# The last twelve batches of a gathered low-rank residual kernel, written out as one list

## The chip, the cores and the metric

The kernel runs on one core of a Trainium2 chip. Time is the device time of one execution in microseconds (us); the median of three runs before the change is 304.21 us (304.19 to 304.54). A core has a matrix engine (TensorE, PE in the profile), VectorE (DVE), ScalarE (ACT), GpSimd (POOL) and SyncE (SP), each with an instruction queue of its own, and 16 DMA engines. SBUF is the on-chip memory, PSUM the eight banks into which TensorE writes.

## The reference: what is computed

Each of B = 128 batches has S = 128 rows of H = 512 numbers and an index that picks one of L = 10 parameter sets.

```python
w1 = W1[language_ids]                                   # 512 x 128 for each batch
w2 = W2[language_ids]                                   # 128 x 512
h = relu(einsum('bsh,bha->bsa', x, w1) + b1[ids])
y = x + einsum('bsa,bah->bsh', h, w2) + b2[ids]
normed = (y - mean(y)) * rsqrt(var(y) + 1e-5)           # over H
out = x + normed * gamma[ids] + beta[ids]
```

Everything is float32.

## The kernel before, in words

One batch is one tile of 128 partitions (its rows) by 512 columns. x is loaded four batches at a time, results are stored two at a time (tile o). A batch b passes through these steps, each a function of the kernel:

- `transpose_x` (TensorE, four 128x128 transposes into PSUM) and `copy_xT` (ScalarE, back to SBUF);
- `stage_w1` (ScalarE, copies the batch's W1 from the ten that stay in SBUF into a small tile, because the index is known only on the chip);
- `down` (TensorE, four products) and `relu` (ScalarE);
- `up` (TensorE, one product of 512 columns into one of five PSUM banks, `py`);
- `add_b2` and `add_beta` (GpSimd: r = x + b2, o = x + beta). For some batches VectorE (`vector_b2`) or, for the last two, TensorE adds b2 instead;
- `residual` (VectorE: py += r, with the row sum as a by-product) and `square` (ScalarE: sum of squared deviations);
- `scalar_means` and `deviation` (ScalarE: minus the mean, and an approximate 1/sqrt, the root, into a PSUM bank that rotates), then `rstd` in three small VectorE steps that sharpen the root by Newton's method. Means, roots and rstd are made for two batches (a pair) at once;
- `scale` (VectorE: (py - mean) * gamma) and `finish` (VectorE: py * rstd + o, into o), then `store` (SyncE).

The function `keep` makes each engine issue in exactly the order in which the code is written, so the text is the schedule. The main loop (line 577) writes one batch per turn, with the stages of about five batches interleaved: x is turned two batches ahead, a batch is finished about two behind. With E = 123, batches 124 to 127 are handled by `tail(b)` (line 463): there mean, root and rstd are made for one batch alone (`deviation_of`, `rstd_of`, `of_one` with the roots of 126 and 127 in PSUM banks of the finished stages), and the ends of 123, 124 and 125 leave VectorE: `by_pool` lets ScalarE make n = py * rstd + shift and GpSimd multiply by gamma (for 123 and 124) and add it to o. 125 to 127 are stored singly or in halves, some of it from ScalarE's queue (`store_last`).

Of the kernel before, what the change touches and what calls it, by code (L numbers as in the profile page):

```python
# [26 lines left out]
def cond_resid_kernel(ctx: ExitStack, tc: tile.TileContext, x, itok, W1, b1, W2, b2, gamma, beta, out):  # L27
# [112 lines left out]
    def lid(b, engine):  # L140
        g = b // G
        if (g, engine) not in lids:
            loads, vals = nc.values_load_multi_w_load_instructions(
                lang[0:1, g * G : (g + 1) * G],
                engines=[engine],
                min_val=0,
                max_val=L - 1,
                skip_runtime_bounds_check_because="clamped on the chip to 0..L-1 above",
            )
# [164 lines left out]
    def col(tiles, b):  # L314

        return tiles[b // 2][:, b % 2 : b % 2 + 1]
# [43 lines left out]
    def root(ssq, t):  # L360
        keep(nc.scalar.activation(t, ssq, AF.Abs_reciprocal_sqrt, bias=eps, scale=1.0 / H3))  # L361

    def newton(n, ssq, t, u):
        if n == 1:
            keep(nc.vector.scalar_tensor_tensor(u, ssq, EPS * H3, t, ALU.add, ALU.mult))  # L365
        else:
            keep(nc.vector.scalar_tensor_tensor(u, u, 1.0 / H3, t, ALU.mult, ALU.mult))

    def newton_3(rstd, t, u):
        keep(nc.vector.scalar_tensor_tensor(rstd, u, -3.0, t, ALU.add, ALU.mult))  # L370
# [28 lines left out]
    def finish(b):  # L399
        g, j = divmod(b, 2)  # L400
        o = os[g][:, j, :]
        keep(
            nc.vector.scalar_tensor_tensor(o, ys.pop(b), rstds[g][:, j : j + 1], o, ALU.mult, ALU.add)  # L403
        )

    def store(g):
        keep(nc.sync.dma_start(out=out[2 * g : 2 * g + 2].rearrange("b s h -> s b h"), in_=os.pop(g)))
        del rstds[g]

    def on(b):  # L410
        return 0 <= b < B
# [3 lines left out]
    shifts = {}  # L415
    halves = slice(0, H // 2), slice(H // 2, H)

    def of_one(b):
        if -b not in parts_of:
            pool, tag = {E + 3: (p_h, "h"), E + 4: (p_x, "xT")}.get(b, (p_s, "s"))  # L420
            parts_of[-b] = pool.tile([P, 1], FP, tag=tag, name=f"root_of_{b}"), st.tile([P, 1], FP, tag="part", name=f"part_of_{b}")
        return parts_of[-b]

    def rstd_of(b, n):

        t, u = of_one(b)
        if n < 3:
            newton(n, ssqs[b], t, u)
        else:
            rstds[b] = st.tile([P, 1], FP, tag="rstd", name=f"rstd_{b}")  # L430
            newton_3(rstds[b], t, u)

    def deviation_of(b):
        ssqs[b] = st.tile([P, 1], FP, tag="ssq", name=f"ssq_{b}")
        sq = tp.tile([P, H], FP, tag="sq", name=f"sq_{b}")
        keep(nc.scalar.activation(sq, ys[b], AF.Square, bias=col(sums, b), scale=-float(H), accum_out=ssqs[b]))  # L436
        root(ssqs[b], of_one(b)[0])

    def rstd_col(b):
        return rstds[b] if b > E else rstds[b // 2][:, b % 2 : b % 2 + 1]  # L440
# [5 lines left out]
    def by_pool(b, scaled, cols=slice(0, H)):  # L446

        n = rp.tile([P, H], FP, tag="r", name=f"n_{b}")[:, cols]
        bias = 0.0 if scaled else shifts[b]
        keep(nc.scalar.activation(n, ys[b][:, cols], AF.Identity, bias=bias, scale=rstd_col(b)))  # L450
        if not scaled:
            keep(nc.gpsimd.tensor_tensor(n, n, gamma_b[:, bass.ds(lid(b, ET.Pool) * H, H)], ALU.mult))
        for part in halves if b > E else (cols,):
            keep(nc.gpsimd.tensor_tensor(os[b // 2][:, b % 2, part], n[:, part], os[b // 2][:, b % 2, part], ALU.add))
# [4 lines left out]
    def finish_cols(b, cols=slice(0, H)):  # L459
        o = os[b // 2][:, b % 2, cols]  # L460
        keep(nc.vector.scalar_tensor_tensor(o, ys[b][:, cols], rstd_col(b), o, ALU.mult, ALU.add))  # L461

    def tail(b):
        p = E // 2
        residual(b)
        if b == E + 1:
            rstd(p, 1)
            scale(E - 1)
            rstd(p, 2)
            finish(E - 2)  # L470
            store(p - 1)
            rstd(p, 3)
            deviation_of(b)
            shift(E)
            by_pool(E, False)
        elif b == E + 2:
            rstd_of(b - 1, 1)
            negative_means(b // 2)
            rstd_of(b - 1, 2)
            finish_cols(E - 1)  # L480
            store_last(E - 1)
            rstd_of(b - 1, 3)
            store_last(E)
            deviation_of(b)
        elif b == E + 3:
            left, right = slice(0, H // 2), slice(H // 2, H)
            few, most = slice(0, H // 4), slice(H // 4, H)
            shift(b - 2)
            by_pool(b - 2, False)
            residual(b + 1)  # L490
            rstd_of(b - 1, 1)
            scale(b - 1)
            rstd_of(b - 1, 2)
            deviation_of(b)
            negative_means(b // 2)
            scale(b)
            rstd_of(b - 1, 3)
            rstd_of(b, 1)
            deviation_of(b + 1)
            rstd_of(b, 2)  # L500
            by_pool(b - 1, True)
            for part in halves:
                store_last(b - 2, nc.scalar, part)
            for part in halves:
                store_last(b - 1, nc.scalar, part)
            rstd_of(b, 3)
            rstd_of(b + 1, 1)
            finish_cols(b)
            store_last(b)
            rstd_of(b + 1, 2)  # L510
            scale(b + 1)
            rstd_of(b + 1, 3)
            for cols in (left, right):
                finish_cols(b + 1, cols)
                store_last(b + 1, nc.sync, cols)


    def spin(n, width):
        idle = p_s.tile([P, H], FP, tag="s", name="idle")
# [54 lines left out]
    up(1)  # L574

    turned = 5
    for i in range(3, B + U):
        b = i - U - 1
        if b > G and b % G == 2 and b // G + 3 < NG and b // G + 3 >= 5:
            load_x(b // G + 3)  # L580
        up_to = i
        if b <= E:
            if turned <= up_to and on(turned):
                transpose_x(turned)
            add_b2(b + 2)
# [18 lines left out]
        if b == E:  # L604
            add_b2(b + 3)
            add_beta(b + 1)
            add_b2(b + 4)
            for n in range(b + 2, B):
                add_beta(n)
        if b > E:  # L610
            tail(b)
        elif half == 0:
            if on(b):
                vector_b2(b)
                residual(b)
                square(b)
            if mine:
                scale(2 * p)
                rstd(p, 1)
            if old:  # L620
                finish(2 * p - 1)
                store(p - 1)
        else:
            if on(b):
                vector_b2(b)
            if mine:
                rstd(p, 2)
            if on(b):
                residual(b)
                square(b)  # L630
            if mine:
                rstd(p, 3)
                scale(2 * p + 1)
            if mine:
                finish(2 * p)
        if 0 <= g and b <= E and half == 1:
            scalar_means(g)
            deviation(g)

        for n, engine in ((turned + 2, ET.Activation), (i - U + 3, ET.PE), (b + 1, ET.DVE), (b + 6, ET.Pool)):  # L640
            if on(n):
                lid(n, engine)


# [35 lines left out]
```

## Time and profile before

| | |
|---|---|
| median of three runs | 304.21 us |
| the profiled execution | 304.08 us, its span 302.3 us |
| busy share of the span | TensorE 96%, VectorE 97%, ScalarE 92%, GpSimd 94% |
| granted TensorE clock | 0.993 on the mean |
| HBM traffic | 43.3 MB read, 33.6 MB written, 254 GB/s over the span |
| one turn of the loop (from one `up` to the next) | 2.19 us |
| last `up` starts, last VectorE instruction ends, span ends | 292.40, 299.20, 302.3 us |

Times in views count from the start of the span. The busy shares are averages over the whole run; what bounds the end must be read from the end. A busy time is that of an instruction from its start to its end; on VectorE the next one starts some 0.09 us before the one ahead has ended, so the cost of an instruction to its engine is the distance from its start to the next start. "SPq" and "ACTq" are the queues of SyncE and ScalarE that issue transfers.

### The profile page before, as it was taken

How to read it: one execution, taken by the hardware profiler on the slowest of the kernel's cores; microseconds unless marked ns; L12 is line 12 of the kernel's file. 1: busy time of each engine (PE TensorE's matmuls, PEld its weight loads, DVE VectorE, ACT ScalarE, POOL GpSimd, SP SyncE). 2: the span in 40 equal slices, each digit the busy share in tenths (PEclk: the TensorE clock that was granted, in tenths of full speed). 3: DMA queues.
4: the chain of work that ended last, by engine and by line, in shares of the span. 5: the costliest groups of instructions: out<-in, count | busy, mean ns of one | idle time of the engine just before them, and what ended most of it. 6: DMA issues, size and time to landing. Idle time of an engine off the chain costs nothing.

```text
span 302.3 us, 7001 instructions
## 1 busy us (share of the span) xinstructions
PE 290.6 (96%) x1820; PEld 218.0 (72%) x1821; DVE 294.2 (97%) x784; ACT 279.6 (92%) x771; POOL 284.9 (94%) x240
## 2 busy tenths in 40 slices
PE   7899999999999999999999999999999999999980
PEld 3758787777777777777777777777777777777740
DVE  6989999999999999999999999999999999999995
ACT  5878789999999999999999999999999999999982
POOL 1299998999999999999999999999999999999995
PEclk9999999999999999999999999999999999999997
DMA  6999999986667876766678667767866666882244
GB/s 235 385 389 364 346 339 402 404 307 206 233 234 243 279 255 205 244 209 261 222 280 270 212 204 240 263 226 261 279 211 221 218 253 217 271 283 113 108 166 173
DMA packets 43929, 77.33 MB, mean 256 GB/s; under 512 B 2121, under 2 KB 8020, under 8 KB 43890
## 3 DMA queue, kind: packets, MB, share of 16 engines
q1 hardware_dynamic: 43254, 76.31, 73.5%
q10 hardware_dynamic: 636, 0.57, 0.6%
q8 instruction: 15, 0.25, 0.3%
q14 instruction: 24, 0.20, 0.2%
HBM read 43.32 MB, written 33.55 MB: 254 GB/s over the span
## 4 chain that ended last, share of the span: by engine, by line
PE 89%; DVE 5%; DMA 2%; issue 1%; ACT 1%; SPq 0%; POOL 0%; DVEq 0%; ACTq 0%; POOLq 0%
PE ph L294 36%; PE py L311 35%; PE pxT L271 18%; DMA x<-in_x_dram 2%; DVE py L394 2%; DVE py L328 1%; DVE o L403 1%; PE row L229 1%; SPq L161 0%; ACT n L450 0%; ACT sq L351 0%; ACT sq L436 0%; DVE o L461 0%; ACT w1s L262 0%; DVE rstd L370 0%
## 5 line engine op out<-in xcount | busy, mean ns | idle before, releaser
L288 POOL TENSOR_TENSOR o<-x,beta_b 128x512 f32<-128x512 f32 x128 | 170.1, 1359 | 12.7 <-DVE beta_b L247 11.6
L294 PE MATMUL ph<-xT,w1s 128*128 128x128 f32 x1024 | 135.3, 275 | 0.2 <-DMA w1s<-in_L_cond_W_dram 0.2
L281 POOL TENSOR_TENSOR r<-x,b_b 128x512 f32<-128x512 f32 x97 | 131.7, 1360 | 0.0
L311 PE MATMUL py<-w,hT 128*128 x256 | 131.3, 595 | 0.0
L294 PEld LDWEIGHTS ph<-xT,w1s 128*128 128x128 f32 x1024 | 124.8, 192 | 1.3 <-issue 0.6
L271 PEld LDWEIGHTS pxT<-ident,x 128*128 128x128 f32 x512 | 66.0, 149 | 66.8 <-issue 49.9
L394 DVE SCALAR_TENSOR_TENSOR py<-py,nmean,gamma_b 128x512 f32<-128x512 f32 x126 | 94.8, 753 | 0.0
L403 DVE SCALAR_TENSOR_TENSOR o<-py,rstd,o 128x512 f32<-128x512 f32 x122 | 91.1, 747 | 0.0
L351 ACT ACTIVATE sq<-py,sum 128x512 f32<-128x512 f32 x124 | 85.8, 692 | 0.6 <-DVE py L328 0.6
L275 ACT COPY xT<-pxT 128x512 f32<-128x512 f32 x128 | 74.7, 583 | 4.3 <-PE pxT L271 4.1
L271 PE MATMUL pxT<-ident,x 128*128 128x128 f32 x512 | 77.6, 274 | 0.8 <-DMA x<-in_x_dram 0.6
L262 ACT COPY w1s<-w 128x512 f32 x111 | 68.0, 613 | 0.0
L328 DVE SCALAR_TENSOR_TENSOR py<-py,r 128x512 f32<-128x512 f32 x97 | 66.9, 690 | 0.2
L302 ACT ACTIVATE hT<-ph,b1T 128x128 f32<-128x128 f32 x128 | 46.9, 367 | 8.8 <-PE ph L294 4.2
L311 PEld LDWEIGHTS py<-w,hT 128*128 128x128 f32 x256 | 39.1, 192 | 1.4 <-issue 0.7
L351 ACT ACTIVATION_READ_ACCUMULATOR sq<-py,sum 128x1 f32 x124 | 25.1, 202 | 0.0
L328 DVE SCALAR_TENSOR_TENSOR py<-py,x 128x512 f32<-128x512 f32 x31 | 21.7, 699 | 1.4 <-PE py L311 1.1
L321 DVE TENSOR_TENSOR py<-py,b_b 128x512 f32<-128x512 f32 x27 | 18.6, 689 | 0.1
L361 ACT ACTIVATE root<-ssq,eps 128x2 f32<-128x2 f32 x62 | 16.5, 265 | 0.0
L328 DVE DVE_READ_ACCUMULATOR py<-py,r 128x1 f32 x97 | 13.6, 140 | 0.0
L342 ACT ACTIVATE nmean<-sum 128x2 f32<-128x2 f32 x62 | 12.3, 198 | 0.0
L365 DVE SCALAR_TENSOR_TENSOR part<-ssq,root 128x2 f32<-128x2 f32 x62 | 9.3, 149 | 0.2 <-ACT root L361 0.2
(57 smaller groups left out, 81.2 us busy)
## 6 DMA issues: line engine op xcount, KB each, us to landing
out_dram<-o SPq DMA_DIRECT2D x61, 512.0 KB, 3.3
x<-in_x_dram SPq DMA_DIRECT2D x27, 1024.0 KB, 6.7
x<-in_x_dram SPq DMA_DIRECT2D x10, 512.0 KB, 7.2
w1s<-in_L_cond_W_dram SPq DMA_DIRECT2D x17, 256.0 KB, 8.7
w<-in_L_cond_W_dram SPq DMA_DIRECT2D x4, 640.0 KB, 8.2
w<-in_L_cond_W_dram SPq DMA_DIRECT2D x1, 1792.0 KB, 9.8
w<-in_L_cond_W_dram SPq DMA_DIRECT2D x1, 768.0 KB, 5.3
out_dram<-o SPq DMA_DIRECT2D x3, 256.0 KB, 2.0
```

Of the source, the lines that this page charges most:

```text
L262: keep(nc.scalar.copy(w1s[b].rearrange("p k a -> p (k a)"), src))
L271: keep(nc.tensor.transpose(pxs[b][:, k, :], cols, ident))
L275: keep(nc.scalar.copy(xT[b], pxs.pop(b)))
L281: keep(nc.gpsimd.tensor_tensor(rs[b], xb(b), b2_b[:, bass.ds(v * H, H)], ALU.add))
L288: keep(nc.gpsimd.tensor_tensor(os[g][:, j, :], xb(b), beta_b[:, bass.ds(v * H, H)], ALU.add))
L294: nc.tensor.matmul(phs[b], lhsT=w1s[b][:, k, :], rhs=xT[b][:, k, :], start=(k == 0), stop=(k == KC - 1))
L302: keep(nc.scalar.activation(hT[b], phs.pop(b), AF.Relu, bias=b1T[:, bass.ds(lid(b, ET.Activation), 1)]))
L311: keep(nc.tensor.matmul(ys[b], lhsT=hT[b], rhs=w2[:, bass.ds(v * H, H)], start=not m, stop=True))
L328: nc.vector.scalar_tensor_tensor(ys[b], ys[b], 1.0, r, ALU.mult, ALU.add, accum_out=col(sums, b))
L351: nc.scalar.activation(sq, ys[b], AF.Square, bias=col(sums, b), scale=-float(H), accum_out=col(ssqs, b))
L394: nc.vector.scalar_tensor_tensor(ys[b], ys[b], col(nmeans, b), gamma_b[:, bass.ds(v * H, H)], ALU.add, ALU.mult)
L403: nc.vector.scalar_tensor_tensor(o, ys.pop(b), rstds[g][:, j : j + 1], o, ALU.mult, ALU.add)
```

## The change

The loop stops after batch 121 has been turned (`range(3, B - 6)`), `tail` goes, and what is left of the twelve batches 116 to 127 is written out as one list of single steps, each on its engine. The work of a batch and the number of VectorE's large instructions stay; these parts change:

- the order of all steps from there on, TensorE's, ScalarE's, VectorE's, GpSimd's and SyncE's; the loads of the indices into registers (`lid`) for the last batches stand together ahead of the list;
- W1 of 125, 126 and 127 comes from HBM by the batch's index (`load_late`, SyncE) instead of by ScalarE's copy;
- by ScalarE and GpSimd go the ends of 120 and 124 (`n_of`, `gamma_of`, `add_of`) instead of 123 and 124; 122 and 123 are ended by VectorE as a pair;
- 125: VectorE writes (py - mean) * gamma to SBUF (`scale_out`), ScalarE makes a diagonal matrix of rstd (`diag_of`), TensorE puts x + beta into a PSUM bank (`base_of`: a product that picks beta's row, and x times the identity) and adds diag times n to it (`product_of`), ScalarE copies the bank to o (`copy_out`);
- 127: x + beta comes from TensorE in the same way and VectorE's last instruction reads it from PSUM;
- the roots of 125 and 126, not of 126 and 127, lie in banks of the finished stages; the means of 124 and 125 are made singly by VectorE, those of 126 and 127 by ScalarE;
- all stores go through SyncE: 120 to 123 as pairs, 124 in halves, 126 and 125 whole, 127 in halves.

```diff
-    for i in range(3, B + U):
+    for i in range(3, B - 6):
...
+    def base_of(b, pool, tag):
+        base[b] = pool.tile([P, H], FP, tag=tag, name=f"base_{b}")
+        pick_b = pick[:, bass.ds(lid(b, ET.PE), 1)].to_broadcast([96, P])
+        keep(nc.tensor.matmul(base[b], lhsT=pick_b, rhs=parts[:96, :], start=True, stop=False))
+        keep(nc.tensor.matmul(base[b], lhsT=ident, rhs=xb(b), start=False, stop=True))
+
+    def end_of(b, cols=slice(0, H)):
+        o = out_of(b)[:, cols]
+        keep(nc.vector.scalar_tensor_tensor(o, (rs if b in base else ys)[b][:, cols], rstd_col(b), base[b][:, cols] if b in base else o, ALU.mult, ALU.add))
...
+        if engine is nc.scalar:
+            keep(nc.scalar.activation(diags[b], ident, AF.Identity, scale=rstd_col(b)))
...
+    def product_of(b, cols=slice(0, H)):
+        keep(nc.tensor.matmul(base[b][:, cols], lhsT=diags[b], rhs=rs[b][:, cols], start=False, stop=True, skip_group_check=True))
+
+    def copy_out(b, cols=slice(0, H)):
+        keep(nc.scalar.copy(out_of(b)[:, cols], base[b][:, cols]))
+
+    def load_late(b):
+        w1s[b] = wp.tile([P, KC, A], FP, tag="w1s", name=f"w1s_{b}")
+        src = W1[bass.ds(lid(b, ET.SP), 1)].rearrange("o (k p) a -> p (o k) a", k=KC)
+        keep(nc.sync.dma_start(out=w1s[b], in_=src))
...
+    lid(E - 3, ET.DVE)
+    lid(E + 1, ET.DVE)
+    lid(E + 1, ET.PE)
+    lid(E + 1, ET.SP)
+    rstd(E // 2 - 3, 2)
+    transpose_x(E - 1)
+    b2_of(E - 2)
+    down(E - 2)
+    up(E - 3)
+    copy_xT(E - 1)
+    residual(E - 4)
+    square(E - 4)
+    rstd(E // 2 - 3, 3)
+    relu(E - 2)
...
+    b2_of(E + 2)
+    load_late(E + 2)
...
+    residual(E + 1)
+    up(E + 2)
+    rstd(E // 2, 3)
+    end_of(E - 1)
+    residual(E + 2)
+    square_of(E + 1)
+    root_of(E + 1)
+    down(E + 4)
+    rstd_of(E + 1, 1)
+    rstd_of(E + 1, 2)
+    square_of(E + 2)
+    up(E + 3)
+    mean_of(E + 1, nc.vector)
+    rstd_of(E + 1, 3)
+    shift(E + 1)
+    end_of(E)
+    relu(E + 4)
+    up(E + 4)
+    mean_of(E + 2, nc.vector)
+    n_of(E + 1, False)
+    residual(E + 3)
+    scale_out(E + 2)
+    root_of(E + 2)
+    store_pair(E // 2 - 1)
+    square_of(E + 3)
+    root_of(E + 3)
+    mean_of(E + 3, nc.scalar)
+    rstd_of(E + 2, 1)
+    residual(E + 4)
+    store_pair(E // 2)
+    rstd_of(E + 2, 2)
+    rstd_of(E + 3, 1)
+    gamma_of(E + 1)
+    add_of(E + 1, halves[0])
+    rstd_of(E + 2, 3)
+    diag_of(E + 2, nc.scalar)
+    rstd_of(E + 3, 2)
+    base_of(E + 2, p_y, "y")
+    add_of(E + 1, halves[1])
+    square_of(E + 4)
+    scale(E + 3)
+    mean_of(E + 4, nc.scalar)
+    store_last(E + 1, nc.sync, halves[0])
+    base_of(E + 4, p_y, "y")
+    rstd_of(E + 3, 3)
+    end_of(E + 3)
+    product_of(E + 2)
+    store_last(E + 1, nc.sync, halves[1])
+    store_last(E + 3, nc.sync)
+    root_of(E + 4)
+    rstd_of(E + 4, 1)
+    copy_out(E + 2)
+    store_last(E + 2, nc.sync)
+    rstd_of(E + 4, 2)
+    scale_out(E + 4)
+    rstd_of(E + 4, 3)
+    end_of(E + 4, halves[1])
+    store_last(E + 4, nc.sync, halves[1])
+    end_of(E + 4, halves[0])
+    store_last(E + 4, nc.sync, halves[0])
```

More of the change, by code (lines that the diff above doesn't have):

```diff
@@ L463, in tail @@
[L463 to L515, printed above, removed]
@@ L603, in cond_resid_kernel @@
         mine, old = 0 <= p < B // 2, 0 <= p - 1 < B // 2
[L604 to L612, printed above, removed]
+        if half == 0:
             if on(b):
@@ L642, in cond_resid_kernel @@
                 lid(n, engine)
+    lid(E - 3, ET.DVE)
[12 more added lines that the diff above has]
+    relu(E - 2)
+    deviation(E // 2 - 2)
+    b2_of(E + 2)
+    load_late(E + 2)
+    transpose_x(E)
+    scale(E - 6)
+    end_of(E - 7)
+    residual(E - 3)
+    stage_w1(E)
+    beta_of(E - 1)
@@ new lines, in cond_resid_kernel @@
+    scalar_means(E // 2 - 2)
+    copy_xT(E)
+    rstd(E // 2 - 2, 1)
+    end_of(E - 6)
+    scale(E - 5)
+    down(E - 1)
+    up(E - 2)
+    rstd(E // 2 - 2, 2)
+    beta_of(E + 1)
+    load_late(E + 3)
+    transpose_x(E + 1)
+    relu(E - 1)
+    down(E)
+    stage_w1(E + 1)
+    copy_xT(E + 1)
+    transpose_x(E + 2)
+    load_late(E + 4)
+    b2_of(E - 1)
+    scale(E - 4)
+    rstd(E // 2 - 2, 3)
+    beta_of(E - 2)
+    square(E - 3)
+    b2_of(E)
+    store_pair(E // 2 - 3)
+    up(E - 1)
@@ new lines, in cond_resid_kernel @@
+    relu(E)
+    residual(E - 2)
+    end_of(E - 5)
+    end_of(E - 4)
+    copy_xT(E + 2)
+    down(E + 1)
+    square(E - 2)
+    up(E)
+    residual(E - 1)
+    transpose_x(E + 3)
+    scalar_means(E // 2 - 1)
+    deviation(E // 2 - 1)
+    rstd(E // 2 - 1, 1)
+    rstd(E // 2 - 1, 2)
+    relu(E + 1)
+    b2_of(E + 1)
+    square(E - 1)
+    scale(E - 2)
+    rstd(E // 2 - 1, 3)
+    residual(E)
+    copy_xT(E + 3)
+    square(E)
+    deviation(E // 2)
+    beta_of(E)
+    end_of(E - 2)
+    down(E + 2)
@@ new lines, in cond_resid_kernel @@
+    up(E + 1)
+    beta_of(E + 3)
+    transpose_x(E + 4)
+    negative_means(E // 2)
+    relu(E + 2)
+    down(E + 3)
+    shift(E - 3)
+    store_pair(E // 2 - 2)
+    scale(E - 1)
+    n_of(E - 3, False)
+    copy_xT(E + 4)
+    rstd(E // 2, 1)
+    relu(E + 3)
+    scale(E)
+    gamma_of(E - 3)
+    add_of(E - 3)
+    rstd(E // 2, 2)
+    residual(E + 1)
[7 more added lines that the diff above has]
+    rstd_of(E + 1, 1)
```

91 lines of the change are left out of this document (61 added, 30 removed).

## The prediction, made before the result was known

> **What bounds the kernel now.** I read the page's shares first, then the busy time by stretch of the end, then VectorE's timeline there, then the stores.
>
> ```profile
> PE 290.6 (96%) x1820; PEld 218.0 (72%) x1821; DVE 294.2 (97%) x784; ACT 279.6 (92%) x771; POOL 284.9 (94%) x240
> ```
> ```profile
> core 0: us, PE busy (x) PEld busy (x) DVE busy (x) ACT busy (x) POOL busy (x), PEclk, DMA share, GB/s
> 278.00:285.00 7.00, 7.00 (x49) 5.42 (x48) 7.00 (x19) 6.82 (x21) 7.00 (x7) 1.00 0.40 153
> 285.00:289.00 4.00, 4.00 (x27) 2.95 (x26) 3.91 (x11) 3.91 (x12) 4.00 (x4) 1.00 0.35 133
> 289.00:293.50 4.50, 4.47 (x21) 2.37 (x19) 4.25 (x18) 3.88 (x12) 4.00 (x5) 1.00 0.30 117
> 293.50:299.20 5.70, 0.00 (x0) 0.00 (x0) 5.34 (x19) 3.28 (x8) 5.22 (x6) 0.93 0.46 174
> ```
> To 289 us everything is full, and TensorE sets the pace. After 293.5 TensorE has nothing left and VectorE works to 299.20. So a new order of the end can win only VectorE's waits and what comes behind VectorE. The prices are in its timeline (columns: start, duration, engine, line, operation):
>
> ```profile
> 278.56 0.75 DVE L394 SCALAR_TENSOR_TENSOR py<-py,nmean,gamma_b 128x512 f32<-128x512 f32 x1
> 279.22 0.75 DVE L403 SCALAR_TENSOR_TENSOR o<-py,rstd,o 128x512 f32<-128x512 f32 x1
> 279.89 0.69 DVE L328 SCALAR_TENSOR_TENSOR py<-py,r 128x512 f32<-128x512 f32 x1
> 280.50 0.14 DVE L328 DVE_READ_ACCUMULATOR py<-py,r 128x1 f32 x1
> ...
> 289.25 0.16 DVE L365 SCALAR_TENSOR_TENSOR part<-ssq,root 128x2 f32<-128x2 f32 x1 [0.19 <-ACT root L361]
> 289.38 0.76 DVE L394 SCALAR_TENSOR_TENSOR py<-py,nmean,gamma_b 128x512 f32<-128x512 f32 x1
> ...
> 296.04 0.15 DVE L365 SCALAR_TENSOR_TENSOR part_of<-ssq,root_of 128x1 f32<-128x1 f32 x1
> 296.22 0.16 DVE L367 SCALAR_TENSOR_TENSOR part_of<-part_of,root_of 128x1 f32<-128x1 f32 x1
> 296.41 0.15 DVE L370 SCALAR_TENSOR_TENSOR rstd<-part_of,root_of 128x1 f32<-128x1 f32 x1
> 296.48 0.15 DVE L365 SCALAR_TENSOR_TENSOR part_of<-ssq,root_of 128x1 f32<-128x1 f32 x1
> 296.67 0.75 DVE L461 SCALAR_TENSOR_TENSOR o<-py,rstd,o 128x512 f32<-128x512 f32 x1
> ...
> 298.06 0.15 DVE L370 SCALAR_TENSOR_TENSOR rstd<-part_of,root_of 128x1 f32<-128x1 f32 x1
> 298.32 0.88 DVE L461 SCALAR_TENSOR_TENSOR o<-py,rstd,o 128x256 f32<-128x256 f32 x2
> ```
> From start to start a scaling costs 0.66 us, a final product and add 0.66, a residual 0.61 (its accumulator's read lies inside), an independent small step 0.07, one that needs its predecessor 0.18, and a big one behind a fresh rstd 0.26.
>
> ```profile
> GB/s 0 0 18 0 164 378 378 246 0 0 0 0 0 0 0 355 396 382 32 319 264 0 0 168 382 32 0 0 273 196 371 344 342 339 339 128 0 0 0 0
> ...
> out_dram<-o SPq DMA_DIRECT2D x2, 512.0 KB, 2.8
> out_dram<-o SPq DMA_DIRECT2D x3, 256.0 KB, 2.0
> out_dram<-o ACTq DMA_DIRECT2D x4, 128.0 KB, 2.2
> out_dram<-o SPq DMA_DIRECT2D x2, 128.0 KB, 2.1
> ```
> These are the transfers of 285 to 303 us, 0.45 us a column. Columns 31 to 35, 298.5 to 300.7, are full at 339 to 371 GB/s: the last five stores lie on each other, and the 128 KB ones take 2.1 to 2.2 us where a lone 256 KB store takes 2.0.
>
> **The change part by part.** *VectorE.* From 277.82 (second Newton step of pair 58) to 299.20 it spends 21.38 us. Big work: 9 residuals x 0.61 + 9 scalings x 0.66 + 8 whole ends x 0.66 + two halves 0.88 = 17.59. The new list has the same 9, 9, 8 and 2: the batches that leave VectorE for GpSimd are 120 and 124 instead of 123 and 124, and 125's end leaves it again. So nothing big is saved; what differs is the remaining 3.79 us of small steps and waits.
>
> Before, by start times: 0.06 to 0.10 at twelve places, 0.85 together; 0.18 ahead of 288.30 (waits for TensorE); 0.47 ahead of 289.38 (pair 61's root); 0.31 at 290.77; 0.31 at 291.69; 0.18 ahead of 293.51 (shift and TensorE); 0.45 from 294.86 to 295.31 (a mean behind ScalarE); 0.69 from 295.98; 0.26 at 298.06. Sum 3.70.
>
> After, laying the new list out engine by engine, each instruction at the later of its engine and its inputs: nine independent steps 0.63; pair 60's root and dependent step 0.35; mean of 61 with the shift of 120 0.18; end of 122 behind its rstd 0.26; 124's three steps, mean and shift ahead of the end of 123 0.64; the interleaved steps of 125 and 126 0.34; end of 126 0.26; 127's first two steps 0.25; its halves 0.26. Sum 3.17, 0.5 less. TensorE does not enter: by its 2.19 us a batch (275.5 to 289 us), plus 0.25 where down(122) now waits for hT of 121, the second product of 127 is done near 293.8, and the residual of 127 starts at 294.1, after VectorE's own queue; that margin is 0.1 to 0.3 us for each of 122 to 127.
>
> The new list puts two register loads on VectorE's sequencer between the end of 115 and the Newton step at 277.82; of the old ones each stood alone:
>
> ```profile
> L143 DVEq TENSOR_LOAD <-lang x5: 610/619/998, 252.7 to 286.9; - x5
> ```
> One of 0.62 us cost the engine nothing at 278.70 (the ends around it stay 0.66 apart), since the sequencer runs ahead of the engine. Two are 1.24 us. Bounds: 0, and 1.24 if nothing hides them. The nearest row is the hidden one, and the two instructions ahead are a scaling and an end, 1.3 us of work: I take 0.1. VectorE nets -0.4. SyncE and TensorE get a load too (0.30 to 0.33 us), behind work that is due over 1 us later.
>
> *Late W1.* ScalarE loses three copies (3 x 0.51) and one scaling onto n (0.68), and gains diag (0.27, by the 128x128 relu) and 125's copy (0.49, by the xT copy): 1.5 us less on an engine that is not last. SyncE gains three loads ahead of store 58. Landing rows for such loads are 4.2 to 10.2 us, the long ones from the crowded start. Issued near 279, the first lands by 289.2 at worst and 283.2 at best; down(125) is due at 286.9. Here the queue runs at 150 GB/s, so I take the short end: 0; the other end is 2.3 us of TensorE's stall.
>
> *GpSimd.* 14 full passes where there were 17 (1.24 each): it ends near 296 instead of 298.8. It reads batch 125 at 278 instead of 285; that x load is issued at 264.7 and lands in 7 us. *TensorE* gains two bf16 products (0.22 each) and three f32 ones of 512 columns (0.86 each), all after its last batch: 3.0 us, to 296.8; the diag for the third is there at 295.5. Then 125's copy ends at 297.5 and its store issues near 297.7. Cover: VectorE's last half, at 298.8; the cover ends if the product slips by 0.8 us.
>
> *Stores.* Before, one store of 256 KB and four of 128 KB move after 298.3, and the last, issued at 299.26, lands 2.1 us later. After, 125's goes as one of 256 KB and is through by 299.3; 127's halves are issued near 298.5 and 298.9 with nothing ahead. Lone stores: 512 KB 2.8 us, 256 KB 2.0, so 1.2 us and 3.1 us per MB, or 1.6 to 1.65 for 128 KB (estimate from these two rows) against 2.1 now. Bounds: 0 gain (all rows with 128 KB) and 0.5. I take 0.45, since no other store is then open. All stores now go through SyncE at 0.33 to 0.40 us of issue each; the spacing of the last four (0.4 us and more) leaves room. Store 60 now waits for GpSimd's add of 120 (near 291.9) with store 61 behind it, which is ready only at 292.8.
>
> "DMA: Bandwidth & Descriptors" of the Trainium skill (section "Anatomy of one DMA — SWDGE (gpsimd) path") gives another path's DMA a fixed 2.0 us plus bytes by 436 GB/s; that is 2.3 us for 128 KB, and by it the last store would not land sooner and the time would be 303.8. The trace speaks against it as far as 256 KB in 2.0 us goes.
>
> Sum: 304.08 (the profiled execution; its span 302.3 and 1.78 around it) - 0.5 + 0.1 - 0.45 = 303.23. The median shown, 304.21, is 0.13 above that execution: 303.4.
>
> **The rivals.** *Only VectorE gains*, the last store still takes 2.1 us: 304.21 - 0.4 = 303.8. For it: every 128 KB row. Against: those rows overlap other stores.
>
> *The list only trades waits.* 0.4 us of VectorE's gain goes to TensorE's margin: if up(123) or up(125) is more than 0.15 us later than laid out, each residual behind waits. Stores gain at most 0.2: 304.0 to 304.2. For it: margins of 0.1 to 0.3 against layout errors of the same size.
>
> *The two register loads stall VectorE* at 277.8 (slower than before). Price 1.24 us, less the hidden part; it decides once 0.9 us of it shows, which eats the whole gain. In full: 303.3 (the forecast without its 0.1) + 1.24 = 304.6. For it: GpSimd's own loads take 0.79 us when they meet VectorE's. Against: 278.70.
>
> *W1 of 125 lands late*: TensorE waits up to 2.3 us for 289.2, VectorE with it from 125's residual on, less its 0.2 margin: 303.4 + 1.4 to 2.1 = 304.8 to 305.5. Against: an idle queue.
>
> **How the numbers follow.** Forecast 0.50 (303.4; own range 303.0 to 303.7), only VectorE 0.17, trading 0.15, register loads 0.10, late W1 0.05, more than forecast (below 303.0) 0.03. Leaving out the late load and what lies below 302.9, the range is 302.9 to 304.6. A measurement of this kernel tells about 0.2% from no change, 0.61 us: faster means below 303.60, slower above 304.82. Faster: 0.43 of the forecast's 0.50, 0.07 of the second, 0.03 = 0.53. Slower: late W1 0.05, half of the register loads 0.05, and 0.04 for what the trace does not show = 0.14. The rest, 0.33, is the same.
>
> **What would show it.** Right: VectorE's last half ends near 298.8 with its gaps behind 284 at 0.26 or less; the last 128 KB store lands in 1.7 us; 125's copy ends by 297.8. Wrong: a gap at 277.8 (register loads), TensorE weight loads that wait for the W1 transfer at 287, residuals of 122 to 127 that wait for TensorE, or a last store of 2.1 us. A product at half clock (the row from 293.50 has 0.93) would cost 0.86 us on 125's store and reach the end only through SyncE's order.

## The result, and the profile after

The changed kernel takes 303.38 us (median of 9 runs, 303.13 to 303.69), the kernel before 304.30 us beside it (median of 9, 304.19 to 305.11). The ratio is 0.9967, with a 95% interval of 0.9958 to 0.9976: 0.9 us less. The profiled execution took 303.50 us, its span is 301.7 us.

No busy share on the page has moved by more than a point:

```profile
PE 294.0 (97%) x1829; PEld 219.4 (73%) x1829; DVE 294.1 (97%) x785; ACT 278.9 (92%) x770; POOL 281.2 (93%) x236
```

The busy time by stretch of the end, same columns as before (time, then busy us and instructions of each engine, granted clock, DMA share, GB/s):

```profile
278.00:285.00 7.00, 7.00 (x47) 5.33 (x46) 7.00 (x20) 6.42 (x18) 7.00 (x7) 1.00 0.80 259
285.00:289.00 4.00, 4.00 (x27) 2.95 (x26) 3.97 (x15) 3.60 (x13) 4.00 (x4) 1.00 0.37 141
289.00:293.50 4.50, 4.50 (x26) 2.96 (x25) 4.37 (x16) 3.96 (x11) 2.67 (x3) 1.00 0.10 35
293.50:299.10 5.60, 3.56 (x10) 1.26 (x8) 5.34 (x19) 3.30 (x12) 2.68 (x3) 1.00 0.78 292
```

TensorE works on behind 293.5 (the two bases and 125's product), at a granted clock of 1.00 where the row of before had 0.93. ScalarE has 0.4 us more idle time in the first stretch and 0.3 in the second; that will matter below.

The point from which the two programs differ on VectorE is the second Newton step of pair 58. It starts at 277.82 us before and at 278.16 after: this execution fell behind among the first loads, where the programs are the same (its first scaling is already 0.32 us late), and kept that. So everything at the end is read from that step on, called the fork below. VectorE's timeline there (start, duration, engine, line, operation):

```profile
278.16 0.14 DVE L367 SCALAR_TENSOR_TENSOR part<-part,root 128x2 f32<-128x2 f32 x1
...
285.57 0.14 DVE L328 DVE_READ_ACCUMULATOR py<-py,r 128x1 f32 x1
285.60 0.16 DVE L365 SCALAR_TENSOR_TENSOR part<-ssq,root 128x2 f32<-128x2 f32 x1
...
286.65 0.69 DVE L328 SCALAR_TENSOR_TENSOR py<-py,r 128x512 f32<-128x512 f32 x1
...
291.65 0.15 DVE L365 SCALAR_TENSOR_TENSOR part_of<-ssq_of,root_of 128x1 f32<-128x1 f32 x1
...
292.36 0.74 DVE L488 SCALAR_TENSOR_TENSOR o<-py,rstd,o 128x512 f32<-128x512 f32 x1
...
297.90 0.15 DVE L370 SCALAR_TENSOR_TENSOR rstd_of<-part_of,root_of 128x1 f32<-128x1 f32 x1
298.16 0.87 DVE L488 SCALAR_TENSOR_TENSOR o<-n,rstd_of,base 128x256 f32<-128x256 f32 x2
```

From the fork to the end of the last half VectorE takes 299.03 - 278.16 = 20.87 us; before it was 21.38: 0.51 less. The longest stretch of small steps that is left is 0.71 us, 291.65 to 292.36, the single steps of 124.

The transfers of 285 to 303 us, 0.45 us a column, with the issues (count, size, median us from issue to landing):

```profile
GB/s 41 23 319 364 387 118 0 0 0 0 36 0 0 0 0 0 0 0 373 360 387 382 391 387 50 98 194 262 184 373 373 264 253 260 71 0 0 0 0 0
...
out_dram<-o SPq DMA_DIRECT2D x3, 512.0 KB, 3.0
out_dram<-o SPq DMA_DIRECT2D x4, 128.0 KB, 1.7
out_dram<-o SPq DMA_DIRECT2D x2, 256.0 KB, 2.0
```

128 KB now take 1.7 us in the median, against 2.1 and 2.2 before. By the trace's raw record of SyncE the wait on the last store is passed 1.78 us after its issue (issued 299.09, passed 300.87), before 2.14 us (299.26, 301.40): 0.36 less. From that wait to the end of the span it is 0.87 us where it was 0.93: 0.06 less.

So the gain has three pieces, -0.51 on VectorE, -0.36 in the last store, -0.06 behind it, together -0.93 from the fork to the end. The two spans lie 0.58 us apart, and with the 0.34 us by which the second execution came late to the fork that is the 0.92 between the medians.

### The profile page after: what moved, and what is told of

The parts are those of the page before. It is cut to its first block, busy times and chain, and to the rows that moved or that the text cites. A ratio compares the mean times of both kernels' runs of the same rounds, so it can differ in the third digit from the quotient of the medians.

```text
span 301.7 us, 7025 instructions
## 1 busy us (share of the span) xinstructions
PE 294.0 (97%) x1829; PEld 219.4 (73%) x1829; DVE 294.1 (97%) x785; ACT 278.9 (92%) x770; POOL 281.2 (93%) x236
## 4 chain that ended last, share of the span: by engine, by line
PE 89%; DVE 5%; issue 2%; DMA 2%; SPq 0%; POOL 0%; DVEq 0%; POOLq 0%
PE ph L294 36%; PE py L311 35%; PE pxT L271 18%; DMA x<-in_x_dram 2%; DVE py L328 1%; DVE o L488 1%; DVE py L394 1%; PE row L229 1%; DVE n L494 0%; SPq L161 0%; PE py L310 0%; SPq L143 0%; PE idle L529 0%; DVE rstd_of L370 0%; DVEq L826 0%
## 5 line engine op out<-in xcount | busy, mean ns | idle before, releaser
L288 POOL TENSOR_TENSOR o<-x,beta_b 128x512 f32<-128x512 f32 x121 | 163.1, 1380 | 12.6 <-DVE beta_b L247 11.6
L281 POOL TENSOR_TENSOR r<-x,b_b 128x512 f32<-128x512 f32 x92 | 127.1, 1382 | 0.0
L394 DVE SCALAR_TENSOR_TENSOR py<-py,nmean,gamma_b 128x512 f32<-128x512 f32 x124 | 93.5, 754 | 0.0
L403 DVE SCALAR_TENSOR_TENSOR o<-py,rstd,o 128x512 f32<-128x512 f32 x116 | 86.8, 748 | 0.0
L262 ACT COPY w1s<-w 128x512 f32 x108 | 66.1, 612 | 0.0
L370 DVE SCALAR_TENSOR_TENSOR rstd<-part,root 128x2 f32<-128x2 f32 x62 | 9.4, 152 | 0.0
```

Of the source, the lines that this page charges most:

```text
L262: keep(nc.scalar.copy(w1s[b].rearrange("p k a -> p (k a)"), src))
L281: keep(nc.gpsimd.tensor_tensor(rs[b], xb(b), b2_b[:, bass.ds(v * H, H)], ALU.add))
L288: keep(nc.gpsimd.tensor_tensor(os[g][:, j, :], xb(b), beta_b[:, bass.ds(v * H, H)], ALU.add))
L394: nc.vector.scalar_tensor_tensor(ys[b], ys[b], col(nmeans, b), gamma_b[:, bass.ds(v * H, H)], ALU.add, ALU.mult)
L403: nc.vector.scalar_tensor_tensor(o, ys[b], rstds[g][:, j : j + 1], o, ALU.mult, ALU.add)
```

## The experiments

**How the table is read.** The end of every run is taken from its own fork. "VectorE" is the time from the fork to the start of the last halves' instruction. "Landed" is the time from the last store's issue to the wait that it releases, "place" which of SyncE's eight last waits that is (what it means comes with the last experiment), "to the end" the time from the fork to the end of the span. The ratio is to the kernel before, measured again beside each run (304.25 to 304.42 us), with its 95% interval; each of these is good to about 0.3 us. The profile's columns come from one execution of each kernel, but where two kernels do the same work, their instructions stand at the same distance from the fork within 0.02 us.

| kernel | VectorE | landed | place | to the end | median us | ratio to before |
|---|---|---|---|---|---|---|
| before | 20.50 | 2.14 | 7 | 24.51 | 304.30 | 1 |
| after | 20.00 | 1.78 | 8 | 23.58 | 303.38 | 0.9967 [0.9958, 0.9976] |
| after, W1 by copies | 21.03 | 1.78 | 5 | 24.79 | 304.60 | 1.0015 [1.0005, 1.0026] |
| before, late W1 | 20.26 | 2.09 | 2 | 24.53 | 304.52 | 1.0001 [0.9993, 1.0010] |
| after + 1 on VectorE | 20.74 | 1.77 | 8 | 24.32 | 303.97 | 0.9987 [0.9978, 0.9996] |
| after + 1 on TensorE | 20.81 | 1.77 | 8 | 24.39 | 304.08 | 0.9985 [0.9974, 0.9996] |
| after + 1 on ScalarE | 20.51 | 1.77 | 8 | 24.08 | 304.01 | 0.9992 [0.9983, 1.0001] |
| after + 1 on GpSimd | 20.34 | 1.77 | 8 | 23.91 | 303.61 | 0.9970 [0.9956, 0.9983] |
| before, no stores of 125 | 20.50 | 1.78 | 5 | 24.27 | 304.22 | 0.9994 [0.9985, 1.0004] |
| after, 127 cut 384 + 128 | 20.00 | 1.69 | 8 | 23.63 | 303.52 | 0.9971 [0.9961, 0.9981] |
| after, 125 by GpSimd | 20.27 | 1.77 | 8 | 23.85 | 303.60 | 0.9977 [0.9966, 0.9987] |
| after, beta of 127 by GpSimd | 19.92 | 1.79 | 8 | 23.51 | 303.44 | 0.9969 [0.9957, 0.9980] |
| after, more register loads | 19.99 | 1.77 | 8 | 23.57 | 303.42 | 0.9968 [0.9955, 0.9981] |
| after, 124 late and reordered | 19.87 | 1.81 | 1 | 23.92 | 303.80 | 0.9977 [0.9968, 0.9987] |

**W1 of the last three by ScalarE's copies again.** One part of the change undone:

```diff
-    load_late(E + 2)
-    load_late(E + 3)
-    load_late(E + 4)
+    stage_w1(E + 2)      # behind copy_xT(E + 1)
+    stage_w1(E + 3)      # behind copy_xT(E + 2)
+    stage_w1(E + 4)      # behind copy_xT(E + 3)
```

> The changed kernel with W1 of 125, 126 and 127 by ScalarE's copies again, in place of the three late loads. The prediction costed the relief of ScalarE at nothing, because ScalarE is not last: by that 0. Rival: in the new list ScalarE is full to 290 us, three copies of 0.51 us push the turned x, the relu and the squares back, TensorE and VectorE wait for them: 0.7 to 1.2 us slower, laid out from the rows +1.0, so that without the late loads the list would be no gain at all.

Measured: 304.60 us, slower than the kernel before (304.25 beside it). VectorE is 1.03 us later than in the changed kernel, as the rival said; 0.18 more comes behind the last store. ScalarE's timeline of this kernel, then the same root in the changed kernel:

```profile
282.34 0.59 ACT L275 COPY xT<-pxT 128x512 f32<-128x512 f32 x1 [0.42 <-PE pxT L271]
282.82 0.62 ACT L262 COPY w1s<-w 128x512 f32 x1
283.34 0.69 ACT L351 ACTIVATE sq<-py,sum 128x512 f32<-128x512 f32 x1
...
284.73 0.65 ACT L262 COPY w1s<-w 128x512 f32 x1
285.25 0.72 ACT L351 ACTIVATE sq<-py,sum 128x512 f32<-128x512 f32 x1
...
286.09 0.27 ACT L361 ACTIVATE root<-ssq,eps 128x2 f32<-128x2 f32 x1
...
287.67 0.63 ACT L262 COPY w1s<-w 128x512 f32 x1
```
```profile
285.31 0.27 ACT L361 ACTIVATE root<-ssq,eps 128x2 f32<-128x2 f32 x1
```

The two copies of 0.52 us (start to start) stand ahead of the squares of 120 and 121, and the root of pair 60 starts at 286.09, which is 8.18 us behind this run's fork at 277.91; in the changed kernel it starts at 285.31, 7.15 us behind its fork. VectorE waits for exactly that root there (285.57 to 285.60 in the fence of the result), so nothing is left to take up a delay. The third copy, at 287.67, adds nothing: VectorE is 1.04 us late at that root and 1.03 at the end. The sentence of the prediction that costs this part at nothing is refuted: without the late loads, and with the copies in these places, the new list is no gain but a loss of 0.53 us on VectorE (21.03 against 20.50).

**Late W1 alone, in the old order.** The same part, put into the kernel before:

```diff
-            if on(n + 1) and n + 1 >= FIRST:
+            if on(n + 1) and FIRST <= n + 1 <= E + 1:
                 stage_w1(n + 1)
+            if E + 2 <= n + 3 < B:
+                load_late(n + 3)
```

> The kernel before, its order kept, with W1 of 125, 126 and 127 by late loads in place of ScalarE's three copies: one part of the change alone. Theory, after the run with the copies put back: ScalarE is as tight as VectorE only in the new list, and the old order, in which TensorE's 2.19 us a batch sets the pace to 289 us, can't use the relief: 0 to 0.15 us less than before (laid out from the rows, 0.13). Rival: ScalarE's relief is what pays, in any order: 0.5 us less or more, most of the change's gain. A third way, against both: the loads take the DMA queue from store 58 or from x, and it is slower.

Measured: no change, ratio 1.0001 [0.9993, 1.0010]. The trace shows why it is so little: VectorE gains 0.24 us (20.26 against 20.50; 0.13 had been laid out), and from the landing of the last store to the end it takes 1.25 us instead of 0.93. So the relief of ScalarE is worth 0.24 us on VectorE in the old order and 1.03 in the new one. The two parts of the change belong together: everything but the late loads +0.53, late loads alone -0.24, both -0.50.

**One more instruction on one engine.** Four kernels, each the changed one with one instruction that nobody needs, early in the list:

```diff
     residual(E - 2)
+    keep(nc.vector.scalar_tensor_tensor(more, ys[E - 2], 1.0, xb(E), ALU.mult, ALU.add))
```
```diff
     up(E)
+    keep(nc.tensor.matmul(ys[E], lhsT=again, rhs=w2[:, bass.ds(lid(E, ET.PE) * H, H)], start=True, stop=True))
```
```diff
     copy_xT(E + 2)
+    keep(nc.scalar.copy(more, xb(E)))
```
```diff
+    keep(nc.gpsimd.tensor_tensor(more, xb(E), xb(E - 1), ALU.add))
     b2_of(E + 2)
```

> The changed kernel with one more instruction of VectorE (512 columns, as large as an end, its result unused) right after the residual of 122. Theory: VectorE's queue sets the end, so its own cost of 0.66 us less what waits take up: +0.5 to +0.66 us. Rival: there is slack on VectorE behind TensorE and ScalarE: below 0.2.

> The changed kernel with the second product of batch 123 done twice (0.86 us more of TensorE). Theory: TensorE leads VectorE's residuals of 123 to 127 by only 0.1 to 0.3 us, so 0.6 to 0.8 us of it reach the end. Rival: TensorE is covered as in before, its last product ends 5 us ahead of the end: below 0.3.

> The changed kernel with one more ScalarE copy of 512 columns (0.5 us, result unused) after the turned x of 125. Theory: ScalarE has less than 0.5 us of slack there, about 0.1 us reaches the end. Rival (ScalarE is the tightest engine of the list): 0.3 to 0.5 us. Rival (ScalarE is not last, as predicted): 0.

> The changed kernel with one more GpSimd add of 512 columns (1.24 us, result unused) ahead of b2 of 125. Theory: GpSimd has some 0.9 us of slack in the middle of the list, so about 0.35 us reaches the end through b2 of 121 or beta. Rival: GpSimd was relieved by three passes and covers it: 0. Rival: no slack: 0.8 us and more.

Measured, by VectorE's column against 20.00: VectorE +0.74, TensorE +0.81 of its 0.86, ScalarE +0.51 of its 0.52, GpSimd +0.34 of its 1.24. The times agree within 0.3 us (303.97, 304.08, 304.01 and 303.61 against 303.38). VectorE's own instruction (it stands behind the residual of 121, not of 122 as the expectation has it) cost more than the range expected for it, 0.5 to 0.66. It takes 0.61 us up to the next start (283.49 to 284.10), and 0.17 is a break ahead of it, 283.32 to 283.49, behind the residual whose bank it reads; of these 0.78 the wait for the root of pair 60 takes up 0.04:

```profile
283.32 0.14 DVE L328 DVE_READ_ACCUMULATOR py<-py,r 128x1 f32 x1
283.49 0.69 DVE L693 SCALAR_TENSOR_TENSOR more<-py,x 128x512 f32<-128x512 f32 x1
284.10 1.40 DVE L488 SCALAR_TENSOR_TENSOR o<-py,rstd,o 128x512 f32<-128x512 f32 x2
```

ScalarE's copy was expected at 0.1 and cost all of itself; the expectation that called ScalarE the tightest engine of the list was right. In that run ScalarE goes from 282.45 to 287.4 us without a break:

```profile
284.32 0.65 ACT L696 COPY more<-x 128x512 f32<-128x512 f32 x1
284.84 0.72 ACT L351 ACTIVATE sq<-py,sum 128x512 f32<-128x512 f32 x1
285.42 0.23 ACT L351 ACTIVATION_READ_ACCUMULATOR sq<-py,sum 128x1 f32 x1
285.52 0.23 ACT L342 ACTIVATE nmean<-sum 128x2 f32<-128x2 f32 x1
285.69 0.27 ACT L361 ACTIVATE root<-ssq,eps 128x2 f32<-128x2 f32 x1
```

TensorE's and GpSimd's instructions reach VectorE at the residual of 123, the one at 286.65 in the changed kernel (so GpSimd's not at 121, as expected); first with TensorE's, then with GpSimd's:

```profile
287.60 0.70 DVE L328 SCALAR_TENSOR_TENSOR py<-py,r 128x512 f32<-128x512 f32 x1 [0.72 <-PE py L700]
```
```profile
286.63 0.70 DVE L328 SCALAR_TENSOR_TENSOR py<-py,r 128x512 f32<-128x512 f32 x1 [0.25 <-POOL r L427]
```

What follows: around 285 us three engines bind at once, each with less than 0.1 us to spare for an instruction at these places, and only GpSimd has slack, 0.9 us. Behind 286.65 each of these delays, whoever made it, goes through VectorE to the last half unchanged. That does not mean that VectorE alone bounds all that stands there: a later experiment delays it through ScalarE's last root.

**The last store without 125's.** The kernel before, with two stores less:

```diff
             for part in halves:
                 store_last(b - 2, nc.scalar, part)
-            for part in halves:
-                store_last(b - 1, nc.scalar, part)
```

> The kernel before without the two stores of batch 125 (125's output is missing). Theory: the last store of before takes 2.1 us because other stores lie on it. VectorE still ends at 299.2 us of the span, the last store lands in 1.7 to 1.8 us, and the time falls by 0.3 to 0.4 us, to about 303.9 us. Rival: 128 KB always take about 2.1 us here, and what made the new list's last store shorter is something else (its place in SyncE's queue): landing 2.1 us, time within 0.1 us of before.

Measured: the landing falls from 2.14 to 1.78 us, by the same 0.36 as in the changed kernel, with VectorE's 20.50 unchanged. That 125's stores lie on the last one is thereby shown as the cause; its size alone is not. Whether it is by their bytes or by their queue, ScalarE's, was not separated. Yet the time is 304.22 us, ratio 0.9994 [0.9985, 1.0004]: expected were 0.3 to 0.4 us less, which lies inside that interval, as does no change. The trace finds 0.24 us less from the fork to the end, because 0.12 us are given back behind the landing (1.05 us instead of 0.93).

**127 cut at 384 and 128 columns.**

```diff
-    end_of(E + 4, halves[1])
-    store_last(E + 4, nc.sync, halves[1])
-    end_of(E + 4, halves[0])
-    store_last(E + 4, nc.sync, halves[0])
+    end_of(E + 4, most)                      # columns 0 to 383
+    store_last(E + 4, nc.sync, most)
+    end_of(E + 4, few)                       # columns 384 to 511
+    store_last(E + 4, nc.sync, few)
```

> The changed kernel with 127's end and stores cut at 384 and 128 columns, in place of 256 and 256. VectorE's work is the same but for 0.05 us. Theory by the sizes (1.2 us and 3.1 us per MB): the last store of 64 KB lands in 1.4 us instead of 1.7 and the end comes 0.2 to 0.3 us sooner. Rival: the store of 192 KB issued 0.4 us ahead lies on it, and the last lands in 1.7 us or later: 0 to 0.2 us slower.

Measured: no gain. The transfers of this kernel:

```profile
out_dram<-o SPq DMA_DIRECT2D x1, 192.0 KB, 1.9
out_dram<-o SPq DMA_DIRECT2D x1, 64.0 KB, 1.7
```

Half the bytes save 0.09 us (1.69 against 1.78), not 0.2 to 0.3, and the store is issued 0.14 us later behind the fork than in the changed kernel: SyncE issues it 0.42 us after the one ahead, as there, and the one ahead now comes later. Whether the 64 KB are held up by the 192 KB ahead or by a least time of a store was not separated.

**125 by GpSimd, and beta of 127 by GpSimd.** TensorE's two new jobs, each undone alone:

```diff
-    diag_of(E + 2, nc.scalar)
+    scaled_of(E + 2)                         # ScalarE: n of 125 times rstd
-    base_of(E + 2, p_y, "y")
+    add_of(E + 2, halves[0])
+    add_of(E + 2, halves[1])
-    product_of(E + 2)
-    copy_out(E + 2)
...
     beta_of(E + 3)
+    beta_of(E + 2)
```
```diff
     beta_of(E + 3)
+    beta_of(E + 4)
...
-    base_of(E + 4, p_y, "y")
...
-    scale_out(E + 4)
+    scale(E + 4)
```

> The changed kernel with 125's last step away from TensorE: ScalarE scales n by rstd in place of making the diagonal matrix, GpSimd adds x + beta in two halves. Theory: 125 lies beside VectorE's last work either way; GpSimd gets three more passes, which delay the adds of 124 and the b2 that residuals wait for, and VectorE's last halves start 0.3 us later: 0.2 to 0.4 us slower. Rival A: hidden in full, 0. Rival B: GpSimd's halves end after VectorE, 125's stores lie on 127's, whose landing goes back from 1.8 to 2.1 us: 0.6 us slower or more.

> The changed kernel with x + beta of 127 by GpSimd again (one pass of 1.24 us), and VectorE's last halves reading it from SBUF. Theory: GpSimd has 1.4 us to spare at 292 us and this lies beside VectorE's queue: within 0.1 us of the changed kernel. Rival: GpSimd's pass pushes b2 of 124 or the gamma of 120 back, as one more add did by 0.34 us: 0.3 us slower.

Measured: 125 by GpSimd 303.60 us, VectorE +0.27, landing 1.77 (no collision of stores). The size is the theory's, the path is not: all residuals keep their distance from the fork within 0.02 us, so GpSimd's passes delayed none. The lines are ScalarE's and then VectorE's, of this kernel:

```profile
295.24 0.72 ACT L515 ACTIVATE n<-n,rstd_of 128x512 f32<-128x512 f32 x1 [0.41 <-DVE part_of L367]
295.87 0.67 ACT L463 ACTIVATE sq<-py,sum 128x512 f32<-128x512 f32 x1
...
296.67 0.26 ACT L361 ACTIVATE root_of<-ssq_of,eps 128x1 f32<-128x1 f32 x1
```
```profile
296.02 0.75 DVE L488 SCALAR_TENSOR_TENSOR o<-py,rstd_of,o 128x512 f32<-128x512 f32 x1
296.96 0.15 DVE L365 SCALAR_TENSOR_TENSOR part_of<-ssq_of,root_of 128x1 f32<-128x1 f32 x1 [0.19 <-ACT root_of L361]
```

The scaling of n takes ScalarE 0.63 us (start to start) where the diagonal matrix takes 0.30 in the changed kernel (295.42 to 295.72); it stands ahead of the square of 127, the root of 127 comes later by that, and VectorE waits for the root. Beta of 127 by GpSimd: 303.44 us, VectorE -0.08: no difference that counts. So of TensorE's two new jobs the first is worth about 0.3 us on VectorE's path, because ScalarE has 0.33 us less to do ahead of the last square, and the second nothing. The times alone tell neither from the changed kernel: the intervals overlap.

**More register loads.** Meant to put four loads in a row on VectorE's sequencer:

```diff
     lid(E + 1, ET.DVE)
+    for _ in range(2):
+        lids.pop(((E + 1) // G, ET.DVE))
+        lid(E + 1, ET.DVE)
```

> The changed kernel with two more register loads on VectorE's sequencer ahead of the list, four in a row instead of two. Theory: the sequencer runs ahead of the engine by about the two large instructions queued before (1.3 us), which hid two loads of 0.34 to 0.6 us; four take 1.4 to 2.4 us, so a gap of 0.1 to 1.1 us opens on VectorE at the fork (278.2 us), and 0 to 1.1 us reach the end, most likely 0.4. Rival: the sequencer's lead is longer than that, no gap, 0.

The run does not test it: the two more loads, whose registers nobody reads, are not in the trace. The register loads behind 250 us (count, ns least, median and most, first and last start), of the changed kernel and then of this one:

```profile
L143 DVEq TENSOR_LOAD <-lang x5: 341/607/947, 253.0 to 276.9; - x5
```
```profile
L143 DVEq TENSOR_LOAD <-lang x5: 339/615/918, 253.0 to 277.0; - x5
L143 DVEq EVENT_SEMAPHORE  x2: 21/21/21, 276.8 to 276.9; - x2
```

Still five; two semaphore instructions of 21 ns are all that was added. For the two loads of the change the changed kernel's own trace gives the answer. They run from 276.46 to 276.81 and from 276.88 to 277.23, 0.35 us each (why one took 0.62 at 278.70 in the kernel before is not shown), and the step that stands behind them starts at 278.16, the end of 115 ahead of it having started at 277.50 and taken its usual 0.66. The sequencer was 1.70 us ahead, and 0.93 of that was left.

**W1 of 124 late too, and three steps reordered.** An attempt at a faster list:

```diff
+    load_late(E + 1)
     b2_of(E + 2)
...
-    stage_w1(E + 1)
...
     rstd_of(E + 1, 1)
+    end_of(E)
...
-    end_of(E)
...
+    root_of(E + 2)
     n_of(E + 1, False)
...
-    root_of(E + 2)
...
+    square_of(E + 4)
     diag_of(E + 2, nc.scalar)
...
-    square_of(E + 4)
```

> The changed kernel with W1 of 124 loaded late too (ScalarE 0.5 us less) and three steps reordered at the end: VectorE's end of 123 between the first and second Newton step of 124, ScalarE's root of 125 ahead of n of 124 and its square of 127 ahead of the diagonal matrix. If half a microsecond on ScalarE counts both ways (one copy more cost 0.5 us), it is worth 0.3 to 0.5 us, with 0.1 us from the reordering: about 302.9 us. If TensorE and VectorE bind as tightly, so that relief of ScalarE alone gives nothing: only the 0.1 us of the reordering, about 303.3 us. If W1 of 124, due at 284.6 us, lands later than that: slower by what it lacks, up to 1 us.

Measured: 303.80 us, ratio 0.9977 [0.9968, 0.9987]. By the ratios it is some 0.3 us slower than the changed kernel, though the intervals just overlap; from the fork to the end it is 0.34. VectorE did what the reordering promised and no more, -0.13 us (19.87 against 20.00). Its timeline shows the end of 123 (L488) filling the place between the steps of 124:

```profile
291.69 0.15 DVE L365 SCALAR_TENSOR_TENSOR part_of<-ssq_of,root_of 128x1 f32<-128x1 f32 x1
291.76 0.74 DVE L488 SCALAR_TENSOR_TENSOR o<-py,rstd,o 128x512 f32<-128x512 f32 x1
292.42 0.16 DVE L367 SCALAR_TENSOR_TENSOR part_of<-part_of,root_of 128x1 f32<-128x1 f32 x1
```

The copy less gave nothing: up to the residual of 125 all residuals keep their distance from the fork within 0.02 us. But it is no mirror of the copy more, which cost 0.51. The copy of 124 stands at 281.56 in the changed kernel, ahead of a wait of ScalarE for TensorE; without it that wait is longer by as much. First the changed kernel, then this one:

```profile
281.56 0.61 ACT L262 COPY w1s<-w 128x512 f32 x1
282.59 0.59 ACT L275 COPY xT<-pxT 128x512 f32<-128x512 f32 x1 [0.42 <-PE pxT L271]
```
```profile
282.64 0.59 ACT L275 COPY xT<-pxT 128x512 f32<-128x512 f32 x1 [0.93 <-PE pxT L271]
```

The copy more stood behind that wait, at 284.32 in its run. A copy less behind it was not run; by the 0.03 us that VectorE waits for the root of pair 60 it could give VectorE no more than that there. W1 of 124 came in time (the residual of 124 starts 11.41 us behind the fork, in the changed kernel 11.40). None of the three cases of the expectation has what made the run slower: it comes after the last store, whose landing takes 1.81 us against 1.78. The raw record of SyncE from that store's issue on, start and duration in us, first the changed kernel, then this one:

```
299.092 0.382  DMA_DIRECT2D        last store          299.009 0.404  DMA_DIRECT2D        last store
299.519 0.017  EVENT_SEMAPHORE     wait 1              300.819 0.017  EVENT_SEMAPHORE     wait 1
299.578 0.028  EVENT_SEMAPHORE     wait 2              300.877 0.028  EVENT_SEMAPHORE     wait 2
299.644 0.028  EVENT_SEMAPHORE     wait 3              300.944 0.028  EVENT_SEMAPHORE     wait 3
299.708 0.028  EVENT_SEMAPHORE     wait 4              301.008 0.028  EVENT_SEMAPHORE     wait 4
299.770 0.028  EVENT_SEMAPHORE     wait 5              301.070 0.028  EVENT_SEMAPHORE     wait 5
299.829 0.028  EVENT_SEMAPHORE     wait 6              301.129 0.028  EVENT_SEMAPHORE     wait 6
300.405 0.028  EVENT_SEMAPHORE     wait 7              301.191 0.028  EVENT_SEMAPHORE     wait 7
300.873 0.028  EVENT_SEMAPHORE     wait 8              301.250 0.028  EVENT_SEMAPHORE     wait 8
300.941 0.007  DRAIN                                   301.317 0.007  DRAIN
```

At its end SyncE passes eight waits in a fixed order, each 0.06 us after the one ahead when its transfers have landed. In the changed kernel the last store releases the eighth: the seven others were passed while it was on its way. In this kernel it releases the first, and the seven others come behind it, 0.43 us. The place goes with the number of transfers that the whole program issues, counted in eights: in all the traces the transfers of the whole program signal eight semaphores in turn, and the last waits take these eight in the same order (a pair that two engines issue within 0.02 us stands swapped in two traces). The number is 136 in the changed kernel (2 stores fewer and 3 loads more than before), remainder 0, place 8; 135 before, place 7; 133 with the copies of W1, and 133 before without 125's two stores, place 5; 138 before with late loads, place 2; 137 in this kernel, place 1. In all fourteen traces the place is the one so counted, with 0.87, 0.93, 1.05, 1.25 and 1.30 us from landing to end at places 8, 7, 5, 2 and 1. It was read from these traces; a kernel that changes nothing but the number of transfers was not run. An estimate from these numbers: the reordering without the fourth late load would keep place 8 and take about 303.25 us (303.38 - 0.13); that was not run, and is less than can be told from the changed kernel.

## Why the prediction was right, and where not

- *The time.* 303.4 was forecast, 303.38 measured; by pieces -0.5 + 0.1 - 0.45 were forecast, and -0.51, 0, -0.36 and -0.06 found.
- *VectorE.* -0.5 forecast, -0.51 measured. The big work is the same; of the small steps and waits 3.17 us were laid out, and 20.87 - 17.59 = 3.28 are there, as 3.79 were there before where the list of them came to 3.70. The rival "the list only trades waits" fell with this, but by little: TensorE's margin was put at 0.1 to 0.3 us for each of 122 to 127, and 0.86 us more of TensorE brought 0.81 to VectorE, so it is 0.05 for 123.
- *Late W1 at 0: the step that failed.* "1.5 us less on an engine that is not last" is wrong. ScalarE is last for the root of pair 60, for which VectorE waits 0.03 us; putting the copies back costs 1.03 us on VectorE, and one copy more 0.51. The sum came out all the same because the laid-out list already had ScalarE without the copies: the worth of the relief was inside the -0.5 and was read as VectorE's. The rows of before could have said it: ScalarE is busy 6.82 of 7.00 and 3.91 of 4.00 us there, nearly as full as VectorE. The other half of the step held: by the trace's semaphore record the three loads land 3.1, 3.8 and 4.7 us after their issue (4.2 to 10.2 were taken), W1 of 125 at 282.31, and 125's first product starts at 286.77; the rival of a late load had no ground.
- *The register loads at +0.1.* They cost 0, the lower bound. They took 0.35 us each, not 0.62, and the sequencer was 1.70 us ahead of the step behind them. What the prediction took as the lead, the scaling and the end, is 1.3; the residual's tail came on top.
- *The last store at -0.45.* -0.36 measured: it takes 1.78 us, not 1.6 to 1.65. The line through 512 and 256 KB gives too little below: 128 KB take 1.78, 64 KB 1.69. The reason given, stores on top of each other, is the one that the run without 125's stores shows, and the rival by which the landing stays at 2.1 fell with it. But "no other store is then open" was not so: when the last store was issued at 299.09, by the semaphore record 125's (landed at 299.75) and 127's first half (300.39) were still under way; before, five others were. "DMA: Bandwidth & Descriptors" of the Trainium skill (section "Anatomy of one DMA — SWDGE (gpsimd) path") gives, by an estimate from its fixed 2.0 us and its 436 GB/s, 2.3 us for 128 KB on the path that it describes; the stores here, issued by SyncE, land in 1.78, so its fixed 2.0 us does not carry over to them.
- *What was not in the sum.* The place of the last store among SyncE's last waits, -0.06 here. At the first place it would have been +0.37, and the time 303.8 by an estimate from the 0.43 us between the places; that the forecast holds to 0.1 us is luck on this point, as it is that 0.1 too much for the register loads and 0.09 too much gain in the last store cancel.
- *TensorE's end of 125 and GpSimd.* In this execution's time, which is 0.34 later, the product of 125 starts at 296.04, its copy ends at 297.68 and its store is issued at 297.70; forecast were 296.8 for the product's end, 297.5 and 297.7, and all lie beside VectorE's last work, as said. GpSimd ends at 296.4 (forecast near 296).

## What to carry to other kernels

Where several engines are full in the same stretch, what a relief is worth can't be read from which engine ends last: ask for every engine which instruction of it another one waits for next, and with how much to spare. One instruction more on each engine in turn measures that in four runs, for the place where it stands. One fewer tells nothing if the engine waits for another one right behind it, as ScalarE did here for 0.42 us. And lay the end out to the last wait: by these traces the place of the last store among the last waits, which goes with the number of transfers, is worth up to 0.43 us.

## What the runs showed of the hardware that was not expected

- SyncE's eight last waits are passed in a fixed order at 0.06 us each, and the last store's place among them goes with the number of transfers of this compiled program; from landing to the end of the span 0.87 us at the eighth place, 1.30 at the first.
- Below 256 KB a smaller store saves little time: 64 KB 1.69 us (with 192 KB issued 0.42 us ahead), 128 KB 1.78, 256 KB 2.0, 512 KB 3.0. With five others still under way at its issue the one of 128 KB took 2.14.
- VectorE's sequencer ran 1.70 us ahead of its engine, and two register loads of 0.35 us cost it nothing.
- In all fourteen traces SyncE issued the last store 0.42 us behind the one ahead, in one of them although its data were ready earlier: with 127 cut at 384 columns VectorE had the last piece ready at 299.00 us, and its store, behind one issued at 298.77, went at 299.20.
